# q and k transposed by VectorE in blocks of 32 and carried to their pixels' partitions by DMA, instead of by TensorE; their products one unit later

## The chip, the cores and the metric

The kernel runs on one core of a Trainium2 chip. The core has TensorE (PE, matrix products), VectorE (DVE), ScalarE (ACT), GpSimd (POOL) and SyncE (SP), each working through its own list of instructions in order, and 16 DMA engines that carry out the transfers which SP and ACT issue. The engines wait for each other through semaphores. The time is the device time from the first to the last instruction, in microseconds (us); the median of the runs counts. Less is better.

## The reference, cut to what matters

The input x is one image of 384 channels and 192 x 192 pixels. Two layers follow each other, each added to its input. The part that the change touches is in the first layer, after a group normalisation:

```python
qkv = jnp.einsum('bchw,oc->bohw', x, w_qkv) + b_qkv[None, :, None, None]
hs, ws = (h // DS, w // DS)                                   # DS = 2
qkv = qkv.reshape(b, 3 * c, hs, DS, ws, DS).max(axis=(3, 5))  # 96 x 96 pixels
qkv = lax.conv_general_dilated(qkv, w_dw, (1, 1), 'SAME', feature_group_count=3 * c, ...)
q, k, v = jnp.split(qkv, 3, axis=1)
...
q = q / jnp.clip(jnp.linalg.norm(q, axis=-1, keepdims=True), 1e-12)
k = k / jnp.clip(jnp.linalg.norm(k, axis=-1, keepdims=True), 1e-12)
attn = jnp.einsum('bhcn,bhdn->bhcd', q, k) * temperature[None]
```

So q, k and v are 384 channels each: a 1x1 product over the channels of x, the maximum over 2x2 pixels, and a 3x3 convolution of each channel by itself. The attention is between channels: for each of 8 heads of 48 channels, the product of q and k is a sum over all 9216 pixels. Four softmaxes over the largest entries of each row, weighted, then multiply v. A GELU, an enlargement to 192 x 192 and a 1x1 product finish the first layer; the second takes the signs of the normalised sum, shifts channels sideways and multiplies by the signs of a weight.

## The kernel before, in words

The image is cut into 24 units of 8 rows (1536 pixels) with the 384 channels as 3 blocks of 128 partitions. A unit of x is one load of 2304 KB into one of 8 buffers of the pool `big`. There are four stages:

1. all units are read once for the group sums (0 to 159 us), and the last six read are kept (`kept`);
2. all units again, for q and k (159 to 1408 us): this is the stage of the change;
3. all units a third time for v, with the softmaxes and the attention between (1408 to 1900 us);
4. the end of the first layer and the second layer, with the output (1900 us on).

In stage 2 the loop over units `u` calls `qkv_unit` for six channel blocks `m`: 0 to 2 are q, 3 to 5 are k. For each `m` PE makes three blocks of 512 columns, each of three matmuls over the input channels (line 316; an fp32 matmul shows in the profile as two passes). DVE takes the maximum over 2x2 pixels of each out of PSUM into `pooled` (line 323, three reductions). ACT adds the bias (line 330), and makes the first of nine taps of the 3x3 convolution (line 337) into a tile `dw`; DVE adds the other eight (line 339, eight instructions of 128 x 384). ACT then copies the last two pooled rows for the next unit (line 341) and sums the squares of `dw` for the norms (line 360). A unit gives 4 rows of 96 pixels, 384 columns; the first unit gives 3 rows, the last 5.

The product of q and k sums over pixels, and PE sums over partitions, so both are needed with pixels on the partitions. For each 128 columns, PE transposes the three q blocks into one PSUM tile `tr` and the three k blocks into another (line 367, against an identity matrix), ACT copies each to `qkT` (line 368), and PE makes three products of 144, 192 and 144 columns (line 371) that stay summed in three PSUM banks `gram` over the whole stage. PSUM's eight banks are three for `qkv`, two for `tr`, three for `gram`.

No order is written by hand in stages 1 to 3: a scheduler places each engine's instructions when the kernel is built, and puts the transposes and products of a unit between the matmuls of the next. PE's list has, for instance, the q transposes of a unit among the next unit's first matmuls. The loads of x in stages 2 and 3 stand on SP's list alone, each waiting for its buffer.

Of the kernel before, what the change touches and what calls it, by code (L numbers as in the profile page):

```python
# [10 lines left out]
F32 = mybir.dt.float32  # L11
# [3 lines left out]
BF16 = mybir.dt.bfloat16  # L15
# [3 lines left out]
PSUM = bass.MemoryType.PSUM  # L19

P = 128
C = 384
CT = C // P
# [9 lines left out]
NU = H // UR  # L33
UPX = UR * W
PR = UR // 2
# [5 lines left out]
LEAD = 4  # L41
SLEN = UR * PITCH
HALF = P // 2

STEP = 1584
SAT = [16 + t * STEP + t - SHIFT // 2 for t in range(CT)]
# [13 lines left out]
KEEP = 6  # L60
# [8 lines left out]
HEAD1 = [((t + 1) * P - 1) // HD for t in range(CT)]  # L69
D0 = [h * HD for h in HEAD0]  # L70
DN = [(h1 - h0 + 1) * HD for h0, h1 in zip(HEAD0, HEAD1)]
PAIR = 2 * HD
NP = C // PAIR
Q = P // NP
# [4 lines left out]
def shift_halves():  # L79
# [8 lines left out]
    for t in range(CT):  # L88
        other.append([])
        for h, (d, e) in enumerate(zip(shift[t], (shift[t][1], 0))):  # L90
            n = HALF - len(of[d])
            at[h * HALF : (h + 1) * HALF, t] = of[d][:REST] + of[e][:n] + of[d][REST:]
            of[e] = of[e][n:]
# [8 lines left out]
def pair_rows():  # L102
# [6 lines left out]
    for p in range(NP):  # L109
        v[p * Q : (p + 1) * Q] = p * PAIR + np.stack([i, HD + i, np.where(i < HD - Q, Q + i, 2 * Q + i)], 1)  # L110
    for t in range(CT):
        o[:PAIR, t] = t * PAIR + np.arange(PAIR)
        o[PAIR:, t] = CT * PAIR + t * Q + i
    assert sorted(v.flat) == sorted(o.flat) == list(range(C))
# [28 lines left out]
def conv_preact_kernel(ctx: ExitStack, tc: tile.TileContext, a: dict, out: bass.AP):  # L143
    nc = tc.nc
# [6 lines left out]
    big = ctx.enter_context(tc.tile_pool(name="big", bufs=NBIG))  # L151

    ident = const.tile([P, P], F32, name="ident")
# [18 lines left out]
    def unit(u, pool=big, parts=1):  # L172
        xt = pool.tile([P, CT, UPX], F32, name="xt", tag="big")
        n = CT // parts
        for t in range(0, CT, n):
            nc.sync.dma_start(xt[:, t : t + n], xv[u][:, t : t + n])
        return xt
# [24 lines left out]
    def right(name, bufs=1, stack=att):  # L202
        return stack.enter_context(tc.tile_pool(name=name, bufs=bufs, side="right"))
# [3 lines left out]
    ssq = ap.tile([P, 2 * CT, NU], F32, name="ssq")  # L207
    gsb = ap.tile([P, CT, max(DN)], F32, name="gsb")
    osum = ap.tile([P, CT, NAB], F32, name="osum")
# [4 lines left out]
    kept = {}  # L214
    with tc.tile_pool(name="p1", bufs=1, side="right") as p1, tc.tile_pool(name="p1ps", bufs=2, space=PSUM) as psp:
        stats = [p1.tile([P, CT, BATCH * (UPX // 512) * 6], F32, name=f"stats{i}") for i in range(NB)]
        mv = p1.tile([P, CT, NB, 2], F32, name="mv")
        acc = p1.tile([P, CT, 2, NU // SHARE], F32, name="acc")
        wg = p1.tile([NG, 3 * C], F32, name="wg")
        seen = 0  # L220
        for i in range(NU):
            u = NU - 1 - i
            xt = unit(u, parts=CT if u in (0, NU - 1) else 1)
# [13 lines left out]
            else:  # L237
                b, k = divmod(seen, BATCH)
                seen += 1
                for t in range(CT):  # L240
                    for j in range(UPX // 512):
                        at = (k * (UPX // 512) + j) * 6
# [3 lines left out]
            if u == NU // 2:  # L246

                for m in range(3):
                    ps = psp.tile([NG, C], F32, name="wgps")
# [7 lines left out]
        more = p1.tile([P, CT, 2], F32, name="more")  # L257
        nc.vector.tensor_reduce(more, acc, AX.X, ALU.add)
        sq = p1.tile([P, CT, NB], F32, name="sq0")
# [5 lines left out]
        ps = psp.tile([NG, 2], F32, name="gsps")  # L265
# [10 lines left out]
        ps = psp.tile([P, CT, 2], F32, name="spread")  # L276
# [9 lines left out]
        ps = psp.tile([P, NM], F32, name="bqps")  # L286
# [4 lines left out]
    def padded(pool, n):  # L291


        ts = []
        for m in range(n):
            t = pool.tile([P, PR + 3, WP + 2], F32, name=f"pooled{m}")
            nc.gpsimd.memset(t[:, 0:2, :], 0.0)  # L297
            nc.gpsimd.memset(t[:, 2 : PR + 2, 0:1], 0.0)
            nc.gpsimd.memset(t[:, 2 : PR + 2, WP + 1 :], 0.0)
            nc.gpsimd.memset(t[:, PR + 2 :, :], 0.0)  # L300
            ts.append(t)
        return ts

    def rows(u):

        return (1 if u else 2), (PR if u < NU - 1 else PR + 1)
# [36 lines left out]

    with tc.tile_pool(name="p2w", bufs=1, side="right") as wp, tc.tile_pool(
        name="p2t", bufs=2, side="right"
    ) as tp, tc.tile_pool(name="p2qkv", bufs=3, space=PSUM) as pqkv, tc.tile_pool(
        name="p2tr", bufs=2, space=PSUM
    ) as ptr, tc.tile_pool(name="p2g", bufs=1, space=PSUM) as pg:
        pool = padded(wp, 2 * CT)
        dwo = [wp.tile([P, (PR + 1) * WP], F32, name=f"dw{m}") for m in range(2 * CT)]  # L350
        gram = [pg.tile([P, 512], F32, name=f"gram{t}") for t in range(CT)]
        for u in range(NU):
            xt = kept.pop(u) if u in kept else unit(u)
            lo, hi = rows(u)
            n = hi - lo + 1
            for m in range(2 * CT):
                acc = dwo[m][:, : n * WP]
                qkv_unit(pqkv, xt, u, m, pool[m], [(acc, 0, n)])
                sq = tp.tile([P, (PR + 1) * WP], F32, name="sq", bufs=1)
                nc.scalar.activation(sq[:, : n * WP], acc, AF.Square, accum_out=ssq[:, m, u : u + 1])  # L360
            for c0 in range(0, n * WP, P):
                L = min(P, n * WP - c0)
                qkT = tp.tile([P, 2, C], F32, name="qkT")
                for s in range(2):
                    ps = ptr.tile([P, C], F32, name="tr")
                    for t in range(CT):
                        nc.tensor.transpose(ps[:L, t * P : (t + 1) * P], dwo[s * CT + t][:, c0 : c0 + L], ident)  # L367
                    nc.scalar.copy(qkT[:L, s, :], ps[:L, :])
                first, last = u == 0 and c0 == 0, u == NU - 1 and c0 + P >= n * WP
                for t in range(CT):  # L370
                    nc.tensor.matmul(  # L371
                        gram[t][:, : DN[t]],
                        qkT[:L, 0, t * P : (t + 1) * P],
                        qkT[:L, 1, D0[t] : D0[t] + DN[t]],
                        start=first,
                        stop=last,
                    )
        for t in range(CT):
            nc.vector.tensor_copy(gsb[:, t, : DN[t]], gram[t][:, : DN[t]])

    wpr = ctx.enter_context(tc.tile_pool(name="wpr", bufs=1)).tile([P, CT, C], F32, name="wpr")
    nc.scalar.dma_start(wpr, a["w_projT"].rearrange("(t p) o -> p t o", p=P))
    def softmaxes(p3, psp):
# [22 lines left out]
        for t in range(CT):  # L406
            g = gsb[:, t, : DN[t]]
            nc.vector.tensor_mul(g, g, rk[:, D0[t] : D0[t] + DN[t]])
            nc.vector.tensor_scalar_mul(g, g, rq[:, t : t + 1])
# [74 lines left out]
    def opened(name, bufs, **kw):  # L484
        return end.enter_context(tc.tile_pool(name=name, bufs=bufs, reuse_waits="tile", **kw))
# [19 lines left out]
    with ExitStack() as vs:  # L505
        wp = right("p4w", stack=vs)
        scratch = vs.enter_context(ExitStack())
        p3 = right("p3", stack=scratch)
        pqkv = vs.enter_context(tc.tile_pool(name="p4qkv", bufs=3, space=PSUM))
# [15 lines left out]
        def attention(g):  # L525
# [4 lines left out]
            for t in range(CT):  # L530
                for p in range(NP):
                    rows = slice(p * Q, (p + 1) * Q)
                    nc.tensor.matmul(  # L533
                        pss[p][:PAIR],
                        aT[rows, t, p * PAIR : (p + 1) * PAIR],
                        chunk[c][rows, t, cols],
# [8 lines left out]
        for u in range(NU):  # L545
            xt = unit(u)
# [6 lines left out]
            lo, hi = rows(u)  # L553
            first = PR * u - 2 + lo
            last = first + hi - lo
# [18 lines left out]
        with tc.manual_schedule():  # L574
# [10 lines left out]
            ps = psp.tile([P, P], F32, name="p3ps")[:NG, :1]  # L585
# [4 lines left out]
            ps = psp.tile([P, P], F32, name="p3ps")[:, :CT].unsqueeze(2)  # L590
# [6 lines left out]
    with end:  # L597
        more, sp = opened("p5x1", 1), opened("p5s", 1)
# [8 lines left out]
        def rows_of(ts, p, at=0, pitch=PITCH, n=W):  # L607
            return ts[p, at : at + UR * pitch].rearrange("p (r w) -> p r w", w=pitch)[:, :, :n]
# [18 lines left out]
        def moved(sg, t, h):  # L627

            d, n = OTHER[t][h]
            p = slice(h * HALF + REST, h * HALF + REST + n)  # L630
            src, to = SAT[t] - HSHIFT[t][h], SAT[t] - d
            by = rest[t % 2]
            nc.gpsimd.tensor_copy(
                rows_of(by.bitcast(I32), p, 0, PITCH // 4, W // 4),
                rows_of(sg.bitcast(I32), p, src // 4, PITCH // 4, W // 4),
            )
            if d:

                assert to % 4 == 0
                nc.gpsimd.tensor_copy(sg.bitcast(I32)[p, to // 4 : (to + SLEN) // 4], by.bitcast(I32)[p])  # L640
            elif to % 2 == 0:
                nc.gpsimd.tensor_copy(
                    rows_of(sg.bitcast(U16), p, to // 2, PITCH // 2, W // 2),
                    rows_of(by.bitcast(U16), p, 0, PITCH // 2, W // 2),
                )
            else:
                nc.gpsimd.tensor_copy(rows_of(sg, p, to), rows_of(by, p))  # L647

        def signed(i):

            xt, sg = kept[order[i]], signs[i % NSIGN]
            for k in range(2 * CT):
                t, h = divmod(k, 2)
                p = slice(h * HALF, (h + 1) * HALF)
                nc.scalar.activation(  # L655
# [47 lines left out]
        with tc.manual_schedule():  # L703
            v = todo.pop(0)
# [85 lines left out]
```

## Time and profile before

The time before is 2334.4 us, the median of three runs (2333.51 to 2335.75); the profiled run has a span of 2331.7 us. Busy time over the span:

| engine | busy us | share | instructions |
|---|---|---|---|
| PE | 2154.3 | 92% | 6573 |
| DVE | 1824.6 | 78% | 3113 |
| ACT | 878.3 | 38% | 1564 |
| POOL | 209.3 | 9% | 337 |

The groups that the change touches or leans on, over the whole run:

| line, engine | what | count | busy us | mean ns |
|---|---|---|---|---|
| 316 PE | qkv, 128x512 | 3888 | 1700.1 | 593 |
| 367 PE | transposes, 128x128 | 438 | 74.3 | 279 |
| 339 DVE | taps of q and k, 128x384 | 1152 | 709.5 | 616 |
| 323 DVE | maximum over 2x2 | 648 | 443.3 | 685 |
| 368 ACT | copies to qkT, 128x384 | 146 | | 475 |

How to read it: busy time of PE is not time at its peak, and matmuls overlap, so the step from one start to the next says more than the length of one. In a timeline line the columns are start, length (us), engine, line, operation, output<-inputs, shape and count, and in brackets the idle time before it and what ended that. In a line of waits they are who waited for whom, us in total, how often, and the longest. In the windows each stretch has its length, and for each engine its busy time and number of instructions, then the granted clock of PE (1.00 is full), the share of the DMA engines and GB/s.

### The profile page before, as it was taken

To read this page: it belongs to the slowest core of one execution; us is meant where nothing else is said; L and a number is where in the kernel's file an instruction comes from. 1 tells how busy PE (TensorE), PEld (TensorE's weight loads), DVE (VectorE), ACT (ScalarE), POOL (GpSimd) and SP (SyncE) were. 2 spreads that over 40 slices of the span, in tenths; PEclk is the share of its full clock that TensorE was granted. 3 is DMA by queue.
4 is the path that set the end of the run, shared out by engine and by line. 5 is a ranking of instruction groups with operands and counts; after the bars stand their busy time and mean duration, and the time that the engine had idled before them with its cause. 6 is when DMAs were issued, how large, how long until landed. Compare 5 with 4: busy or idle time off the path is not lost.

```text
span 2331.7 us, 19363 instructions
## 1 busy us (share of the span) xinstructions
PE 2154.3 (92%) x6573; PEld 1028.9 (44%) x6573; DVE 1824.6 (78%) x3113; ACT 878.3 (38%) x1564; POOL 209.3 (9%) x337
## 2 busy tenths in 40 slices
PE   1039999999999999999999999999999999999998
PEld 0024444445444444444444444443444444455554
DVE  4657777777777777777777788987787887888998
ACT  5432322223222223322322222225333233497775
POOL 0000000000000000000000000000000000186674
PEclk7569999999999999999999999999999999999999
DMA  9961111121111111110111113105221312289995
GB/s 399 418 269 41 41 41 41 43 79 41 41 41 41 41 41 65 58 41 0 41 41 41 41 41 112 41 0 203 82 81 41 122 41 81 82 325 393 412 411 243
DMA packets 47443, 271.54 MB, mean 116 GB/s; under 512 B 2256, under 2 KB 3568, under 8 KB 47344
## 3 DMA queue, kind: packets, MB, share of 16 engines
q1 hardware_dynamic: 36656, 214.70, 23.6%
q10 hardware_dynamic: 10688, 55.61, 5.9%
q8 instruction: 51, 0.84, 0.1%
q14 instruction: 48, 0.39, 0.0%
HBM read 213.68 MB, written 56.62 MB: 116 GB/s over the span
## 4 chain that ended last, share of the span: by engine, by line
PE 48%; DVE 34%; ACT 9%; DMA 7%; issue 2%; SPq 0%; ACTq 0%; POOLq 0%; POOL 0%; DVEq 0%
PE qkv L316 34%; DVE dw L339 18%; DVE pooled L323 9%; DMA xt<-in_x_dram 6%; PE l1ps L675 5%; DVE chunk L339 4%; PE yps L493 3%; ACT pooled L330 3%; ACT dw L337 3%; PE gram L371 3%; PE ops L533 2%; PE tr L367 2%; DVE xt L502 2%; ACT sq L360 2%; ACT signs L655 1%
## 5 line engine op out<-in xcount | busy, mean ns | idle before, releaser
L316 PE MATMUL qkv<-xt,wq 128*128 128x512 f32 x3888 | 1700.1, 593 | 0.3 <-DVE small L289 0.3
L316 PEld LDWEIGHTS qkv<-xt,wq 128*128 128x128 f32 x3888 | 726.1, 190 | 862.3 <-issue 797.0
L339 DVE SCALAR_TENSOR_TENSOR dw<-pooled,small,dw 128x384 f32<-128x384 f32 (+2 forms) x1152 | 709.5, 616 | 251.4 <-ACT dw L337 226.9
L323 DVE TENSOR_REDUCE pooled<-qkv 128x128 f32<-128x512 f32 x648 | 443.3, 685 | 78.5 <-PE qkv L316 72.2
L339 DVE SCALAR_TENSOR_TENSOR chunk<-pooled,small,chunk 128x384 f32<-128x384 f32 (+3 forms) x696 | 370.8, 547 | 73.4 <-ACT chunk L337 56.0
L341 ACT COPY pooled<-pooled 128x196 f32<-128x196 f32 x207 | 73.7, 356 | 743.4 <-DVE dw L339 520.6
L330 ACT ACTIVATE pooled<-pooled,small 128x384 f32<-128x384 f32 x216 | 133.2, 617 | 331.8 <-DVE pooled L323 331.8
L655 ACT ACTIVATE signs<-xt,nmean 64x1536 fp8e4<-64x1536 f32 x144 | 226.5, 1573 | 64.6 <-PE yps L493 52.1
L675 PE MATMUL l1ps<-signs,wb 128*128 128x384 fp8e4 x864 | 151.5, 330 | 5.5 <-POOL signs L647 4.5
L502 DVE SCALAR_TENSOR_TENSOR xt<-yps,small,xt 128x768 f32<-128x768 f32 x132 | 127.9, 1013 | 25.9 <-PE yps L493 21.3
L493 PE MATMUL yps<-chunk,wpr 128*128 128x384 f32 x396 | 138.2, 495 | 6.7 <-DVE xt L502 6.7
L683 DVE SCALAR_TENSOR_TENSOR xt<-l1ps,small,xt 128x768 f32<-128x768 f32 x144 | 135.7, 1009 | 7.1 <-ACT signs L655 4.0
L360 ACT ACTIVATE sq<-dw 128x384 f32<-128x384 f32 (+2 forms) x144 | 75.3, 523 | 158.1 <-DVE dw L339 158.1
L243 DVE BATCH_NORM_STATS2 stats<-xt 128x6 f32<-128x512 f32 x144 | 87.2, 676 | 58.8 <-DMA xt<-in_x_dram 58.8
L297 POOL MEMSET pooled<- 128x196 f32 x9 | 2.4, 267 | 1402.0 <-PE tr L367 1244.3
L675 PEld LDWEIGHTS <-wb 128*128 128x128 fp8e4 x864 | 84.5, 98 | 74.0 <-issue 16.5
L193 PE MATMUL gsps<-sums,small 128*32 128x2 f32 x6 | 0.5, 196 | 125.8 <-DVE sums L264 125.8
L337 ACT ACTIVATE dw<-pooled,small 128x384 f32<-128x384 f32 (+2 forms) x144 | 100.8, 700 | 30.3 <-PE tr L367 28.1
L493 PEld LDWEIGHTS yps<-chunk,wpr 128*128 128x128 f32 x396 | 73.4, 192 | 62.8 <-PE yps L493 16.4
L234 ACT ACTIVATE junk<-xt 128x1536 bf16<-128x1536 f32 x48 | 71.1, 1482 | 51.0 <-DMA xt<-in_x_dram 49.8
L367 PEld LDWEIGHTS tr<-ident,dw 128*128 128x128 f32 (+2 forms) x438 | 52.2, 140 | 70.5 <-DVE dw L339 31.1
L367 PE MATMUL tr<-ident,dw 128*128 128x128 f32 (+2 forms) x438 | 74.3, 279 | 8.9 <-DVE dw L339 8.1
(117 smaller groups left out, 765.9 us busy)
## 6 DMA issues: line engine op xcount, KB each, us to landing
xt<-in_x_dram SPq DMA_DIRECT2D x83, 2304.0 KB, 13.4
out_dram<-xt ACTq DMA_DIRECT2D x19, 2304.0 KB, 13.8
xt<-in_x_dram SPq DMA_DIRECT2D x18, 768.0 KB, 8.2
out_dram<-xt ACTq DMA_DIRECT2D x9, 768.0 KB, 7.6
out_dram<-xt SPq DMA_DIRECT2D x6, 768.0 KB, 6.6
wq<-in_w_qkvT_dram ACTq DMA_DIRECT2D x1, 1728.0 KB, 15.2
wl<-in_w_projG_dram ACTq DMA_DIRECT2D x1, 576.0 KB, 3.8
wpr<-in_w_projT_dram ACTq DMA_DIRECT2D x1, 576.0 KB, 5.1
```

Of the source, the lines that this page charges most:

```text
L316: nc.tensor.matmul(ps, wq[:, t, m * P : (m + 1) * P], x4[:, t, r0 : r0 + nr, c0 : c0 + ncol], start=(t == 0), stop=(t == CT - 1),)
L323: nc.vector.tensor_reduce(pl[:, 2 + r0 // 2 : 2 + (r0 + nr) // 2, 1 + c0 // 2 : 1 + (c0 + ncol) // 2], ps.rearrange("p (i a j b) -> p i j ...
L330: nc.scalar.activation(new, new, AF.Identity, bias=bq[:, m : m + 1])
L337: nc.scalar.activation(acc2, src, AF.Identity, bias=bdw[:, m : m + 1], scale=wdw[:, m, 0:1])
L339: nc.vector.scalar_tensor_tensor(acc2, src, wdw[:, m, k : k + 1], acc2, ALU.mult, ALU.add)
L360: nc.scalar.activation(sq[:, : n * WP], acc, AF.Square, accum_out=ssq[:, m, u : u + 1])
L367: nc.tensor.transpose(ps[:L, t * P : (t + 1) * P], dwo[s * CT + t][:, c0 : c0 + L], ident)
L493: nc.tensor.matmul(ps, wpr[:, t, m * P : (m + 1) * P], o[:, t, :], start=(t == 0), stop=(t == CT - 1),)
L502: nc.vector.scalar_tensor_tensor(x5[:, m, r], yb, bpr[:, m : m + 1], x5[:, m, r], ALU.add, ALU.add)
L655: nc.scalar.activation(rows_of(sg, p, SAT[t] - HSHIFT[t][h]), xt[p, t, :].rearrange("p (r w) -> p r w", w=W), AF.Sign, bias=nmean1[p, t : ...
L675: nc.tensor.matmul(ps[:, j, : 2 * W], wb[:, t, m * P : (m + 1) * P], rows_of(sg, slice(0, P), SAT[t])[:, r0 + 2 * j : r0 + 2 * j + 2], sta ...
L683: nc.vector.scalar_tensor_tensor(blk, ps[:, :, : 2 * W], bl1[:, m : m + 1], blk, ALU.add, ALU.add)
```

## The change

PE no longer transposes q and k, and ACT no longer copies the results. Instead, as soon as a channel block's taps are done, DVE transposes it in blocks of 32 x 32 (`transposed`): within each group of 32 partitions, 32 channels of 32 pixels become 32 pixels of 32 channels. This leaves the pixels of column group j still on the partitions of their channel group i. DMA then carries each such piece to the partitions 32 j to 32 j + 31 (`moved`): 16 transfers for q after `m` = 2 and 16 for k after `m` = 5, all issued by SP, of pieces of 128 bytes for q and 384 bytes for k. They land in `qkT`, which lies in one of the eight buffers of `big` (`room`), so one fewer is left for x. `products` multiplies a unit's q and k in the middle of the next unit. The slices of k are taken in whole blocks of 32 channels (`B0`, `BN`), so the products have 160, 192 and 160 columns.

What it is for: PE is relieved of the transposes, and the two PSUM banks of `tr` go to `qkv`, which has five. Beside this, `dw` is a tile of two buffers instead of six tiles, the squares' output `sq` is bf16, and loads of x are asked for up to six units ahead (`KEEP`), since their place in SP's list is now among the moves.

```diff
+B = 32
+NBP = P // B
...
+B0 = [d // B for d in D0]
+BN = [-(-(d + n) // B) - b for d, n, b in zip(D0, DN, B0)]
...
-    ) as tp, tc.tile_pool(name="p2qkv", bufs=3, space=PSUM) as pqkv, tc.tile_pool(
-        name="p2tr", bufs=2, space=PSUM
-    ) as ptr, tc.tile_pool(name="p2g", bufs=1, space=PSUM) as pg:
+    ) as tp, tc.tile_pool(name="p2qkv", bufs=5, space=PSUM) as pqkv, tc.tile_pool(
+        name="p2g", bufs=1, space=PSUM
+    ) as pg:
...
+        blocks = wp.tile([P, 2, size], F32, name="blocks")
+        nc.gpsimd.memset(blocks, 0.0)
+        room = big.tile([P, CT, UPX], F32, name="room", tag="big").rearrange("p t n -> p (t n)")
+        qkT = room[:, : 2 * size].rearrange("p (s n) -> p s n", s=2)
...
+        def transposed(u, s, t, acc):
+            n, nk, *_ = of_unit(u)
+            to = blocks[:, s, : nk * C].rearrange("p (j t k c) -> p t k j c", j=NBP, t=CT, c=B)[:, t]
+            full, more = divmod(n * WP // B, NBP)
+            nc.vector.transpose(to[:, :full], acc[:, : full * P].rearrange("p (k j c) -> p k j c", j=NBP, c=B))
+            if more:
+                src = acc[:, full * P : n * WP].rearrange("p (j c) -> p j c", c=B)
+                nc.vector.transpose(to[:, full, :more], src)
+
+        def moved(u, s):
+
+            n, nk, q, k = of_unit(u)
+            for j in range(NBP):
+                src = blocks[:, s, j * nk * CT * B : (j + 1) * nk * CT * B]
+                for i in range(NBP):
+                    at, to = slice(i * B, (i + 1) * B), slice(j * B, (j + 1) * B)
+                    if s == 0:
+                        nc.sync.dma_start(
+                            q[to].rearrange("p t k (i c) -> p i (t k) c", i=NBP)[:, i],
+                            src[at].rearrange("p (m c) -> p m c", c=B),
+                        )
+                    else:
+                        nc.sync.dma_start(
+                            k[to].rearrange("p (t i) k c -> p i t (k c)", i=NBP)[:, i],
+                            src[at].rearrange("p (t m) -> p t m", t=CT),
+                        )
...
         for u in range(NU):
-            xt = kept.pop(u) if u in kept else unit(u)
+            for v in range(u, min(u + KEEP + 1, NU)):
+                if v not in kept:
+                    kept[v] = unit(v)
+            xt = kept.pop(u)
...
             for m in range(2 * CT):
-                acc = dwo[m][:, : n * WP]
+                acc = tp.tile([P, (PR + 1) * WP], F32, name="dw")[:, : n * WP]
                 qkv_unit(pqkv, xt, u, m, pool[m], [(acc, 0, n)])
-                sq = tp.tile([P, (PR + 1) * WP], F32, name="sq", bufs=1)
+                transposed(u, *divmod(m, CT), acc)
+                sq = tp.tile([P, (PR + 1) * WP], BF16, name="sq", bufs=1)
                 nc.scalar.activation(sq[:, : n * WP], acc, AF.Square, accum_out=ssq[:, m, u : u + 1])
-            for c0 in range(0, n * WP, P):
-                L = min(P, n * WP - c0)
-                qkT = tp.tile([P, 2, C], F32, name="qkT")
-                for s in range(2):
-                    ps = ptr.tile([P, C], F32, name="tr")
-                    for t in range(CT):
-                        nc.tensor.transpose(ps[:L, t * P : (t + 1) * P], dwo[s * CT + t][:, c0 : c0 + L], ident)
-                    nc.scalar.copy(qkT[:L, s, :], ps[:L, :])
...
+                if u and m == CT - 1:
+                    products(u - 1)
+                if m % CT == CT - 1:
+                    moved(u, m // CT)
+        products(NU - 1)
```

More of the change, by code (lines that the diff above doesn't have):

```diff
@@ L345, in conv_preact_kernel, with of_unit, products @@
         name="p2t", bufs=2, side="right"
-    ) as tp, tc.tile_pool(name="p2qkv", bufs=3, space=PSUM) as pqkv, tc.tile_pool(
-        name="p2tr", bufs=2, space=PSUM
-    ) as ptr, tc.tile_pool(name="p2g", bufs=1, space=PSUM) as pg:
+    ) as tp, tc.tile_pool(name="p2qkv", bufs=5, space=PSUM) as pqkv, tc.tile_pool(
+        name="p2g", bufs=1, space=PSUM
+    ) as pg:
         pool = padded(wp, 2 * CT)
-        dwo = [wp.tile([P, (PR + 1) * WP], F32, name=f"dw{m}") for m in range(2 * CT)]
         gram = [pg.tile([P, 512], F32, name=f"gram{t}") for t in range(CT)]
+        size = -(-(PR + 1) * WP // P) * C
+        blocks = wp.tile([P, 2, size], F32, name="blocks")
+        nc.gpsimd.memset(blocks, 0.0)
+        room = big.tile([P, CT, UPX], F32, name="room", tag="big").rearrange("p t n -> p (t n)")
+        qkT = room[:, : 2 * size].rearrange("p (s n) -> p s n", s=2)
+        def of_unit(u):
+            lo, hi = rows(u)
+            n = hi - lo + 1
+            nk = -(-n * WP // P)
+            q, k = qkT[:, 0, : nk * C], qkT[:, 1, : nk * C]
+            return (
+                n,
+                nk,
+                q.rearrange("p (t k c) -> p t k c", t=CT, k=nk),
+                k.rearrange("p (b k c) -> p b k c", k=nk, c=B),
+            )
[22 more added lines that the diff above has]
+                            src[at].rearrange("p (t m) -> p t m", t=CT),
+                        )
+        def products(u):
+            n, nk, q, k = of_unit(u)
+            for i in range(nk):
+                L = min(P, n * WP - i * P)
+                for t in range(CT):
+                    nc.tensor.matmul(
+                        gram[t][:, : BN[t] * B],
+                        q[:L, t, i],
+                        k[:L, B0[t] : B0[t] + BN[t], i],
+                        start=u == 0 and i == 0,
+                        stop=u == NU - 1 and i == nk - 1,
+                    )
@@ L356, in conv_preact_kernel @@
             for m in range(2 * CT):
-                acc = dwo[m][:, : n * WP]
+                acc = tp.tile([P, (PR + 1) * WP], F32, name="dw")[:, : n * WP]
                 qkv_unit(pqkv, xt, u, m, pool[m], [(acc, 0, n)])
-                sq = tp.tile([P, (PR + 1) * WP], F32, name="sq", bufs=1)
+                transposed(u, *divmod(m, CT), acc)
+                sq = tp.tile([P, (PR + 1) * WP], BF16, name="sq", bufs=1)
                 nc.scalar.activation(sq[:, : n * WP], acc, AF.Square, accum_out=ssq[:, m, u : u + 1])
-            for c0 in range(0, n * WP, P):
-                L = min(P, n * WP - c0)
-                qkT = tp.tile([P, 2, C], F32, name="qkT")
-                for s in range(2):
-                    ps = ptr.tile([P, C], F32, name="tr")
-                    for t in range(CT):
-                        nc.tensor.transpose(ps[:L, t * P : (t + 1) * P], dwo[s * CT + t][:, c0 : c0 + L], ident)
-                    nc.scalar.copy(qkT[:L, s, :], ps[:L, :])
[L369 to L377, printed above, removed]
+                if u and m == CT - 1:
[3 more added lines that the diff above has]
+        products(NU - 1)
         for t in range(CT):
-            nc.vector.tensor_copy(gsb[:, t, : DN[t]], gram[t][:, : DN[t]])
+            at = D0[t] - B0[t] * B
+            nc.vector.tensor_copy(gsb[:, t, : DN[t]], gram[t][:, at : at + DN[t]])
     wpr = ctx.enter_context(tc.tile_pool(name="wpr", bufs=1)).tile([P, CT, C], F32, name="wpr")
```

## The prediction

> **What bounds the kernel now.** I read first the windows of the stages. 159 to 1408 us is the stage of q and k, the only one the diff touches; 1408 to 1900 is the stage of v.
>
> ```profile
> core 0: us, PE busy (x) PEld busy (x) DVE busy (x) ACT busy (x) POOL busy (x), PEclk, DMA share, GB/s
> ...
> 211.00:1408.00 1197.00, 1187.58 (x3366) 572.36 (x3365) 915.53 (x1530) 356.12 (x830) 2.27 (x14) 1.00 0.12 43
> 1408.00:1900.00 492.00, 490.25 (x1395) 210.69 (x1394) 408.56 (x875) 161.53 (x363) 0.10 (x1) 1.00 0.21 80
> ```
>
> PE is busy 99% at full clock, DVE 76%, the DMA engines 12%. Next, the timeline of PE over one unit, from its first transpose at 464.32 to the next unit's at 515.79: a period of 51.47 us.
>
> ```profile
> 464.32 0.60 PE L367 MATMUL tr<-ident,dw 128*128 128x128 f32 x4
> ...
> 466.36 0.44 PE L367 MATMUL tr<-ident,dw 128*128 128x128 f32 x2 [0.36 <-DVE dw L339]
> ...
> 474.92 1.79 PE L371 MATMUL gram<-qkT 128*128 128x144 f32 x12
> 476.55 0.82 PE L367 MATMUL tr<-ident,dw 128*128 128x128 f32 x6
> 477.21 1.88 PE L316 MATMUL qkv<-xt,wq 128*128 128x512 f32 x4
> 478.93 0.98 PE L371 MATMUL gram<-qkT 128*128 128x144 f32 x6
> 479.74 36.21 PE L316 MATMUL qkv<-xt,wq 128*128 128x512 f32 x84
> 515.79 0.60 PE L367 MATMUL tr<-ident,dw 128*128 128x128 f32 x4
> ```
>
> Start to start, 84 qkv passes take 36.05 us, 0.429 each; a unit has 108 (54 fp32 matmuls, two passes each): 46.35. The 18 products take 1.63 + 0.81 = 2.44. What is left, 2.68 us, is the 18 transposes with their waits. Then the timelines of DVE and ACT around one block's end, and DVE's waits over the stage.
>
> ```profile
> 457.20 0.68 DVE L323 TENSOR_REDUCE pooled<-qkv 128x128 f32<-128x512 f32 x1
> 457.81 0.61 DVE L339 SCALAR_TENSOR_TENSOR dw<-pooled,small,dw 128x384 f32<-128x384 f32 x1
> 459.69 0.62 DVE L339 SCALAR_TENSOR_TENSOR dw<-pooled,small,dw 128x384 f32<-128x384 f32 x1 [1.28 <-ACT dw L337]
> ```
> ```profile
> 457.92 0.62 ACT L330 ACTIVATE pooled<-pooled,small 128x384 f32<-128x384 f32 x1 [1.50 <-DVE pooled L323]
> 458.45 0.52 ACT L360 ACTIVATE sq<-dw 128x384 f32<-128x384 f32 x1
> 458.88 0.19 ACT L360 ACTIVATION_READ_ACCUMULATOR sq<-dw 128x1 f32 x1
> 458.97 0.69 ACT L337 ACTIVATE dw<-pooled,small 128x384 f32<-128x384 f32 x1
> ```
> ```profile
> DVE dw L339 <- ACT dw L337: 218.4, 136, 3.1
> ...
> DVE pooled L323 <- PE qkv L316: 34.0, 47, 3.9
> ```
>
> DVE's 24% idle isn't free room: after each block's third reduction it waits through three ACT steps. Per unit it works 48 taps x 0.61 + 18 reductions x 0.605 = 40.2 us (steps start to start), waits 218.4 / 23.3 units = 9.4 for ACT, and only 34.0 / 23.3 = 1.5 for PE. So PE is the bound with 1.5 us to spare per unit, and any work put on DVE has to fall into the ACT waits.
>
> [...] No transpose of DVE is in this trace. [...] the moves are pieces of 128 and 384 B. The trace has none so short with data: its shortest, 880 B, took 41 ns each on their engine. [...] in the line below 24 packets of 65 ns per engine are 1.6 of the 3.8 us, which leaves 2.2.
>
> ```profile
> wl<-in_w_projG_dram ACTq DMA_DIRECT2D x1, 576.0 KB, 3.8
> ```
>
> **The change, part by part.**
>
> *PE.* The transposes and their waits go: -2.68 us a unit. The products widen from 144, 192, 144 to 160, 192, 160 columns, 512 for 480, so 2.44 becomes 2.60. New PE period: 46.35 + 2.60 = 48.95. The two banks of `tr` go to `qkv`, five instead of three, so PE can run 5 x 2.58 = 12.9 us ahead of DVE. The products wait on eight DMA semaphores; at 0.02 to 0.05 us each (the semaphore events of the trace), hidden or at most 0.4 us a unit; I take them as hidden behind running matmuls.
>
> *DVE.* Six transposes of 128x384 fp32 per unit. Nearest row: a tap of the same shape, 0.61 us. [...] I take 0.6: +3.6 us. Its place decides what this costs. From a third reduction's next issue slot to the first tap DVE needs 1.905 us (0.605 + 1.28, and the 0.02 between), or 1.375 where ACT's square is already behind it. In the built order, between the two stand: for channel blocks 1 and 2 a tap, the transpose and a reduction (1.815, gap 0.09); for block 3 nothing (1.375); for 4 the transpose (gap 0.775); for 5 and 0 a tap and the transpose (gap 0.695 each). Gaps: 3.7. DVE's period: 40.2 + 3.6 + 3.7 = 47.5. At 1.0 us a transpose: 40.2 + 6.0 + 2.3 = 48.5. Both stay under 48.95. ACT loses six copies of 0.475 us a unit, which also delayed the ACT chain.
>
> *Moves.* 16 for q and 16 for k per unit, all on SP's queue with the load of x between them; each holds SP some 0.37 us (the loads' median), and each waits for the landing of the eighth before it. Engine time per unit: 18 pieces for each q move, 6 for each k move, 384 pieces an engine; at 14 ns (880 B in 41 ns and 1536 in 65 give 9 + 0.037 per byte) 5.3 us, at 82 (twice the 880 B packet) 31 us, both under 48.95. What matters is the wait at the products. k's last transpose stands after the third reduction of the next unit, 3 x 2.58 + 1.4 = 9.2 us after PE ends the unit. The 16 k moves take 16 x 0.37 + 2.3 = 8.2, so all has landed at 17.4; PE reaches the products after 28 to 30 matmuls, at 24.1 or later. Seven us to spare; the load of x (issued when PE ends the unit, 8.1 us to land) is mostly through by 9.2. q's moves follow the products and have half a unit. So: off the path.
>
> *The end of the stage.* The last unit has 480 columns: taps of 0.71, and two transpose instructions for each channel block (0.9). From PE's start of that unit, DVE stands at 9.6 after block 0, then has 15 reductions (9.1), 48 taps (34.1), 6 x 0.9 and gaps of 3.0: done at 61.2, which is 12.2 after PE's 48.95. The k moves land 8.2 later, at 20.4. PE has three blocks of v (7.7) ahead of the last products, and then stands for 12.7 us (8 to 18), with the whole v stage, PE-bound at 490.25 of 492, behind it in the queue. The next loads of x, queued behind those moves on SP, arrive before v's second unit.
>
> *Sum.* Before: 159.22 to 1407.07 (v's continuous run on PE), 1247.85, of it qkv 2592 x 0.429 = 1112.5, products 73 column blocks x 0.813 = 59.4, slow clock at the start 1.6, so transposes with waits 74.3. After: 1112.5 + 73 x 0.867 + 1.6 + 12.7 = 1190. Saved 57: 2334.4 - 57 = **2277**.
>
> **Rivals.** *DVE becomes the bound.* For it: the margin is 1.4 us in 49, the period rests on ACT's turns, and a 4-byte transpose isn't in the trace. Against: the gaps take up most of a transpose. At 1.4 us each: 40.2 + 8.4 + 1.4 = 50.0, so 24 x 1.05 = 25 more, and 2 for a longer last lag: 2304. *The moves come late and PE stands at every product.* For it: 32 small DMAs a unit, eight in flight, [...] and SP's in-order queue; against: the 2.2 us fixed part and 7 us of room. If each move took as long to land as the 2304 KB loads (13.4 us), 16 would be two rounds, 26.8: 9.2 + 26.8 - 24.1 = 11.9 us a unit, x 23 = 274: 2551, far slower. Break-even lies where the k moves need 17.4 us, 1.1 each. *The end costs more:* if v's second load and DVE's backlog stretch the stand to 30 us, 2294.
>
> **How the numbers follow.** PE-bound with a short stand 0.60; longer stand at the end 0.10; DVE-bound 0.18; late moves 0.12. Best possible is no stand and nothing exposed, 2264. Range 2262 to 2306 leaves out the late moves and little else. Faster by over 0.2%: 0.87; within: 0.02; slower: 0.11.
>
> **What would show it.** Right: in the q and k stage PE periods near 49.0 us with no idle ahead of the products except the last; DVE transposes of 0.5 to 0.7 us; DVE's waits for ACT falling from 9.4 to about 4 us a unit; k moves landing in 8 to 10 us; one PE idle of 8 to 18 us near 1340. Wrong: PE waiting for DVE's reductions (DVE-bound), or for DMA at each product.

## The result and the profile after

The changed kernel takes 2299.36 us (2297.71 to 2301.02, four runs) beside 2333.95 for the kernel before (2331.95 to 2335.75, four runs): a ratio of 0.9852, 95% interval 0.9835 to 0.9869. It is 34.6 us faster; 57 were forecast, 2277 with a range of 2262 to 2306.

First the windows: the stage of q and k, and the 50 us around its end. Columns as in the prediction.

```profile
211.00:1340.00 1129.00, 1127.40 (x2901) 532.22 (x2900) 985.31 (x1664) 298.73 (x687) 0.00 (x0) 1.00 0.23 62
1340.00:1390.00 50.00, 30.14 (x82) 16.23 (x81) 20.42 (x45) 5.03 (x10) 2.37 (x14) 0.80 0.73 276
```

Over the stage PE now has 1127.40 of 1129 us, 99.9% against 99.2%, although DVE went from 76% to 87%. At the end of the stage it works only 30 of 50 us, and at a mean clock of 0.80. Those are the two findings of this case: a steady part that went as worked out, and an end that didn't.

The timeline of PE over one unit in the steady part:

```profile
479.85 2.77 PE L410 MATMUL gram<-room 128*128 128x160 f32 x18
482.45 46.51 PE L321 MATMUL qkv<-xt,wq 128*128 128x512 f32 x108
528.80 2.77 PE L410 MATMUL gram<-room 128*128 128x160 f32 x18
```

No idle stands in brackets, and from product to product it is 48.95 us: 46.35 for 108 passes and 2.60 for 18 products. Before, it was 51.47.

DVE around a block's end, then its group of transposes over the whole run (count | busy us, mean ns | idle ahead), then its waits from 211 to 1330 us:

```profile
455.77 0.58 DVE L381 STREAM_TRANSPOSE blocks<-dw 128x384 f32<-128x384 f32 x1
457.02 0.62 DVE L344 SCALAR_TENSOR_TENSOR dw<-pooled,small,dw 128x384 f32<-128x384 f32 x1 [0.67 <-ACT dw L342]
...
458.16 1.92 DVE L344 SCALAR_TENSOR_TENSOR dw<-pooled,small,dw 128x384 f32<-128x384 f32 x3
459.99 0.68 DVE L328 TENSOR_REDUCE pooled<-qkv 128x128 f32<-128x512 f32 x1
```
```profile
L381 DVE STREAM_TRANSPOSE blocks<-dw 128x384 f32<-128x384 f32 x138 | 79.3, 575 | 3.2
```
```profile
DVE dw L344 <- ACT dw L342: 86.6, 92, 1.5
DVE pooled L328 <- PE qkv L321: 30.4, 64, 0.9
```

A transpose lasts 0.575 us, and it stands in the gap that ACT's chain leaves: the wait after it is 0.67, where the block shown before waited 1.28. Per unit (1119 / 48.95 = 22.9 of them) DVE waits 3.8 us for ACT, down from 9.4, and still 1.3 for PE.

SP's list in one unit, and the page's line of the moves (KB of each, us from issue to landing):

```profile
464.28 10.22 SPq L399 DMA_DIRECT2D room<-blocks  x16
486.99 10.43 SPq L394 DMA_DIRECT2D room<-blocks  x16
```
```profile
room<-blocks SPq DMA_DIRECT2D x736, 36.0 KB, 2.0
```

Sixteen moves hold SP for 10.2 us, 0.64 each from start to start, not 0.37. The k moves have landed at about 476.5, 3.4 us before the products at 479.85.

Now the end of the stage. PE, then DVE, then SP and ACT:

```profile
1337.05 7.99 PE L321 MATMUL qkv<-xt,wq 128*128 128x512 f32 x18 [1.60 <-DVE pooled L328]
1357.49 6.04 PE L410 MATMUL gram<-room 128*128 128x160 f32 x24 [12.45 <-DMA room<-blocks]
1363.36 1.02 PE L321 MATMUL qkv<-xt,wq 128*128 128x512 f32 x2
1371.80 0.48 PE L198 MATMUL p3ps<-small 128*32 128x1 f32 x6 [7.41 <-DVE gsb L438]
...
1400.15 0.49 PE L460 MATMUL p3ps<-dg,ones 128*128 128x128 f32 x2 [1.61 <-DVE dg L458]
```
```profile
1345.56 0.23 DVE L384 STREAM_TRANSPOSE blocks<-dw 128x96 f32<-128x96 f32 x1
1357.66 1.89 DVE L328 TENSOR_REDUCE pooled<-qkv 128x128 f32<-128x512 f32 x3 [11.87 <-DMA room<-blocks]
...
1369.69 1.35 DVE L575 TENSOR_REDUCE wg<-wl 128x96 f32<-128x1152 f32 x1 [8.24 <-DMA wl<-in_w_projG_dram]
1370.96 0.78 DVE L438 COPY gsb<-gram 128x144 f32<-128x144 f32 x3
```
```profile
1345.66 10.25 SPq L399 DMA_DIRECT2D room<-blocks  x16
1355.96 33.31 SPq L181 DMA_DIRECT2D xt<-in_x_dram  x6
```
```profile
1357.59 0.44 ACTq L574 DMA_DIRECT2D wl<-in_w_projG_dram  x1
```

PE stands 12.45 us for the moves, as foreseen. But DVE waits for the same moves before its first reduction of v, which has nothing to do with q or k; ACT issues the load of `wl` only at 1357.59; and once DVE goes on, it stands another 8.24 us for `wl`, with the copies of `gram` (`gsb`) queued behind it and PE behind those.

The kernel before had a wait of the same kind at this place:

```profile
1405.69 1.29 DVE L323 TENSOR_REDUCE pooled<-qkv 128x128 f32<-128x512 f32 x2 [5.95 <-PE tr L367]
```

There too v's first reductions waited, 5.95 us, until the last reader of a tile of q and k (`dw`, read by the transposes) was done, and `wl` was issued right then, at 1405.68. It cost PE nothing, since PE was busy with those transposes, and `wl` landed in 3.8 us.

### The profile page after: what moved, and what is told of

The parts are those of the page before. It is cut to its first block, busy times and chain, and to the rows that moved or that the text cites. A ratio compares the mean times of both kernels' runs of the same rounds, so it can differ in the third digit from the quotient of the medians.

```text
span 2297.4 us, 19469 instructions
## 1 busy us (share of the span) xinstructions
PE 2104.5 (92%) x6135; PEld 995.6 (43%) x6135; DVE 1903.4 (83%) x3269; ACT 819.2 (36%) x1418; POOL 211.2 (9%) x338
## 4 chain that ended last, share of the span: by engine, by line
PE 75%; DVE 11%; DMA 9%; ACT 2%; issue 1%; SPq 1%; ACTq 0%; POOLq 0%; POOL 0%; DVEq 0%
PE qkv L321 63%; DMA xt<-in_x_dram 6%; PE l1ps L734 4%; DVE chunk L344 4%; PE yps L552 3%; PE gram L410 3%; DVE pooled L328 2%; PE ops L592 2%; DVE xt L561 2%; DVE dw L344 1%; DMA out_dram<-xt 1%; ACT signs L714 1%; DVE stats L248 1%; DMA wl<-in_weightT_dram 1%; DMA wl<-in_w_projG_dram 1%
## 5 line engine op out<-in xcount | busy, mean ns | idle before, releaser
L321 PE MATMUL qkv<-xt,wq 128*128 128x512 f32 x3888 | 1682.8, 594 | 1.9 <-DVE pooled L328 1.6
L321 PEld LDWEIGHTS qkv<-xt,wq 128*128 128x128 f32 x3888 | 736.4, 190 | 922.4 <-issue 824.5
L430 ACT ACTIVATE sq<-dw 128x384 bf16<-128x384 f32 (+2 forms) x144 | 75.3, 523 | 116.9 <-DVE dw L344 116.9
L381 DVE STREAM_TRANSPOSE blocks<-dw 128x384 f32<-128x384 f32 (+1 forms) x144 | 82.0, 569 | 3.5
L410 PE MATMUL gram<-room 128*128 128x160 f32 (+3 forms) x438 | 69.9, 315 | 12.4 <-DMA room<-blocks 12.4
## 6 DMA issues: line engine op xcount, KB each, us to landing
xt<-in_x_dram SPq DMA_DIRECT2D x83, 2304.0 KB, 14.9
wq<-in_w_qkvT_dram ACTq DMA_DIRECT2D x1, 1728.0 KB, 14.9
```

What stands on the lines that cost most here:

```text
L321: nc.tensor.matmul(ps, wq[:, t, m * P : (m + 1) * P], x4[:, t, r0 : r0 + nr, c0 : c0 + ncol], start=(t == 0), stop=(t == CT - 1),)
L410: nc.tensor.matmul(gram[t][:, : BN[t] * B], q[:L, t, i], k[:L, B0[t] : B0[t] + BN[t], i], start=u == 0 and i == 0, stop=u == NU - 1 and i ...
```

## The experiments

The theory after reading this: the tile `blocks` lies in the pool `p2w`, whose memory the v stage takes over for `pooled` and `wl`. So v's first reductions and the load of `wl` wait until the last move has read `blocks`, and `wl`, issued late, arrives behind the loads of x that SP has just issued. Rivals: the moves themselves hold up the end, and two queues would cure it; or DVE or the moves are the bound of the steady part. The times given are medians, each compared with runs of the kernel before on the same chip (2333.1 to 2334.1).

**A pool of its own for `blocks`.**

```diff
-    ) as pg:
+    ) as pg, tc.tile_pool(name="p2b", bufs=1, side="right") as pb:
-        blocks = wp.tile([P, 2, size], F32, name="blocks")
+        blocks = pb.tile([P, 2, size], F32, name="blocks")
```

> Only the memory of the tile blocks changes: it gets a pool of its own, so that the tiles of the v stage (pooled, wl) no longer wait for the last k move to release their memory. In the built order PE then has 7 blocks of v, not 3, ahead of the last products. Theory (the late k moves of the last unit hold PE, DVE and the loads of wl because blocks' memory is shared with the v stage): PE's stand of 12.5 us before the last products shrinks to some 4 us in two pieces, the 7.4 us before the product with small and the 11 us wait for weightT vanish; 2299 - 21 = 2278. Rival (it is the queue of x loads ahead of wl, or the data itself, not the memory): both waits stay, at most 5 us gained, 2294 or more.

2274.77 us, ratio 0.9748 (0.9735 to 0.9762): 24.6 below the changed kernel, without touching a move. The timeline of PE in this run, then DVE after its last transpose:

```profile
1336.96 7.99 PE L321 MATMUL qkv<-xt,wq 128*128 128x512 f32 x18 [1.60 <-DVE pooled L328]
1346.40 10.57 PE L321 MATMUL qkv<-xt,wq 128*128 128x512 f32 x24 [1.45 <-DVE pooled L328]
1357.75 3.71 PE L410 MATMUL gram<-room 128*128 128x160 f32 x24 [0.77 <-DMA room<-blocks]
```
```profile
1345.70 1.85 DVE L328 TENSOR_REDUCE pooled<-qkv 128x128 f32<-128x512 f32 x3
```

The moves are issued and land when they did before (products at 1357.75 instead of 1357.49), but PE now has seven blocks of v ahead of the products instead of three, since DVE reads v's banks at once (1345.70 instead of 1357.66), and the stand is 0.77 us. In this run `wl` is issued at 1345.2, before SP's loads of x (1355.9), and lands in 4.1 us. The clock stays at 1.00 from 1340 to 1390 us. The memory that `blocks` shares is the cause of the loss: with it apart, the stand and the late `wl` are both gone. Whether v's tiles lie on the bytes of `blocks` itself or only in the same pool is not told apart by this.

**The last k moves on two queues**, with `blocks` where the change has it:

```diff
+                    eng = nc.scalar if u == NU - 1 and s and i % 2 else nc.sync
-                        nc.sync.dma_start(
+                        eng.dma_start(
```

> For the last unit alone, every second k move is issued by ACT instead of SP. Theory (16 issues of 0.64 us each on one queue are 10.2 of the 12.2 us between the last transpose and the landing): 8 issues take 5.1, PE's stand falls from 12.5 to about 7.4 us, and the later waits stay; 2299 - 5 = 2294. Rival (the transfers themselves are slow): stand unchanged, 2299.

2297.00, ratio 0.9842 (0.9828 to 0.9855). The stand went from 12.45 to 7.90, about as expected, and the wait of PE for `gsb` grew from 7.41 to 8.42, with `wl` still landing 12 us after its issue. Only 2.4 us of the time went. In the profiled run more was gained up to stage 4, which begins 3.8 us earlier than in the changed kernel (its first product on PE at 1992.52 for 1996.36); but stage 4 took 294.5 us for 292.8. No edit here touches stage 4, and over the profiled runs of this document it takes 290.3 to 294.8 us, so 1 or 2 us between two kernels can come from there alone.

**Both together.** The two edits above.

> The two edits together: blocks in a pool of its own, and the last unit's k moves on two queues. PE has 5 blocks of v ahead of the last products in the built order. Theory: with the memory freed, PE's stand is hidden behind v blocks whether the moves take 12 or 7 us, so as the first edit alone within 3 us: 2276 to 2280. Rival (the two gains add): 2278 - 5 = 2273 or less.

2291.74, ratio 0.9825 (0.9812 to 0.9838). The expectation fell: it is 17 slower than the own pool alone. PE of this run, then the load of `wl` (duration in ns, start of the first and last):

```profile
1369.65 0.48 PE L198 MATMUL p3ps<-small 128*32 128x1 f32 x6 [9.68 <-DVE gsb L439]
```
```profile
L575 ACTq DMA_DIRECT2D wl<-in_w_projG_dram x1: 546/546/546, 1353.1 to 1353.1; - x1
```

ACT had eight moves to issue before `wl`, so `wl` left at 1353.1 instead of 1345.2, after SP had begun its loads of x at 1352.6, and took 13.6 us to land. Tested below with `wl` out of the way.

**Three banks for `qkv` instead of five.** `bufs=5` to `bufs=3` in the pool `p2qkv`.

> As the changed kernel, but qkv has three PSUM banks as before instead of five; two stay unused. Theory (the gain is PE's shorter list; DVE keeps pace with 1.5 us to spare per unit): unit period stays at 48.95 us or up to 49.3, 2299 to 2307. Rival (the two banks, which let PE run further ahead, are the gain): period back to 51 us or more, 2340 or more.

2298.89, ratio 0.9853 (0.9839 to 0.9866): no change, with the same period of 48.95. The freed banks gain nothing in this kernel; what the steady part gains is PE's own time.

**Each transpose done twice.**

```diff
-                transposed(u, *divmod(m, CT), acc)
+                for _ in range(2):
+                    transposed(u, *divmod(m, CT), acc)
```

> Every DVE transpose is done twice, with the same result. From the changed kernel's trace: DVE works 43.8 us of a unit's 48.95, waits 3.8 for ACT and 1.3 for PE; a transpose holds DVE for 0.50 us. Theory (DVE's work falls into its waits for ACT): work 46.8, the waits for ACT shrink to 2.2, sum 49.0, so PE stays the bound or nearly, plus some 4 us at the last unit: 2299 to 2315. Rival (DVE work adds in full): 6 x 0.50 x 24 = 72 more, 2371.

2303.34, ratio 0.9866 (0.985 to 0.9883). DVE's busy time from 400 to 1300 us rises from 785.06 to 841.00, 0.51 us for each added transpose, and its waits for ACT fall from 86.6 to 40.7; PE's period stays at 48.95. The 4 us more come at the end of the stage: PE's wait there for a reduction is 3.54 instead of 1.60, and the last transpose is later.

**Each transpose done three times** (`range(3)`).

> Every DVE transpose is done three times, with the same result. Theory (the waits for ACT are used up and DVE becomes the bound): work 49.8 and the 1.4 us of the one wait that nothing covers, 51.2 us a unit, 2.3 over the present, x 24 and 8 at the end: about 2360. Rival one (DVE work adds in full): 144 more, 2443. Rival two (DVE's 5 us of idle time are free room): 6.0 - 5.1 = 0.9 a unit, 2320.

2320.42, ratio 0.9944 (0.9924 to 0.9964, two runs), far less than the theory gave. It is the number of the second rival, but not by that rival's sum, which had 0.9 us a unit and nothing at the end. The windows of this run, 400 to 1300 us, a piece of DVE's timeline, and PE ahead of one unit's products:

```profile
400.00:1300.00 900.00, 890.60 (x2281) 417.20 (x2281) 859.09 (x1524) 238.69 (x545) 0.00 (x0) 1.00 0.23 61
```
```profile
626.34 0.58 DVE L381 STREAM_TRANSPOSE blocks<-dw 128x384 f32<-128x384 f32 x1
626.85 0.58 DVE L344 SCALAR_TENSOR_TENSOR dw<-pooled,small,dw 128x384 f32<-128x384 f32 x1
627.34 0.57 DVE L381 STREAM_TRANSPOSE blocks<-dw 128x384 f32<-128x384 f32 x1
```
```profile
682.86 2.84 PE L410 MATMUL gram<-room 128*128 128x160 f32 x18 [0.93 <-DMA room<-blocks]
```

PE's period is now 49.60 us in the mean (21 units, 287.30 to 1328.84 us), 0.65 more than in the changed kernel. PE stands 9.4 of 900 us, ahead of the products: the k moves come late because DVE does. DVE's waits for ACT are down to 27.0. So about here DVE becomes the bound, with some 6 us of transposes a unit added. The theory counted them in full, but DVE's busy time rose by only 4.6 us a unit (859.09 / 18.15 units against 785.06 / 18.38). In this order many transposes stand between taps, and a tap there takes 0.49 us from start to start (626.85 to 627.34), where three in a row of one block take 0.61 each (458.16 to 459.99 above). PE ends its last qkv pass of q and k 14.2 us later than in the changed kernel (1349.63 for 1335.45); the rest comes at the end, where PE waits 5.82 us for a reduction before its stand.

**All q moves issued twice** (`moved` called again for q).

> Every q move is issued twice, with the same result: 16 more transfers a unit, 10.3 us more of SP's queue. Theory (q's moves have half a unit of room): the queue is free again before the load of x and k's moves are due, 2299 within 4. Rival (the moves load the DMA engines or SP enough to matter): 2310 or more.

2299.46, ratio 0.9854 (0.984 to 0.9869): the same time as the change. q's moves are hidden: in one unit SP issues the 32 of them from 636.5 to 657.4 us, and k's begin at 660.9. The products stand 6 to 18 passes later in PE's list than in the changed kernel, since the order was worked out anew.

**All k moves issued twice.**

> Every k move is issued twice, with the same result. In the changed kernel k's moves are issued from 464.3 to 474.5 us, land by 476.5, and PE reaches the products at 479.85: 3.4 us of room. Theory: 10.2 us more leaves PE standing 6.9 us at every product, x 23, and 10 more at the end: about 2465. Rival (PE runs ahead through its five banks and hides it): 2299 to 2310.

2310.19, ratio 0.99 (0.988 to 0.992, two runs), not 2465. PE in the steady part is busy 900.00 of 900. SP's 32 k moves now take 21 us, but in this kernel the products stand 32 to 42 passes later in PE's list (14 to 18 us): the scheduler moved them behind the longer transfer, which the expectation had held in place. So the steady margin of 3.4 us isn't a cliff as long as the order is worked out anew; what the same moves cost with the order kept was not tried. At the end there is no later work to move behind, and there the cost shows, in PE:

```profile
1368.91 5.15 PE L410 MATMUL gram<-room 128*128 128x160 f32 x24 [22.28 <-DMA room<-blocks]
```

9.8 us more than 12.45, for 16 moves more: about 0.6 each, once.

**`wl` loaded early**, from a pool of its own opened ahead of stage 2, with `blocks` left in `p2w`:

```diff
+    wlp = right("wlp")
+    wl = wlp.tile([P, CT, C], F32, name="wl")
+    nc.scalar.dma_start(wl, a["w_projG"].rearrange("(t p) o -> p t o", p=P))
...
-        wl = wp.tile([P, CT, C], F32, name="wl")
-        nc.scalar.dma_start(wl, a["w_projG"].rearrange("(t p) o -> p t o", p=P))
```

> As the changed kernel, but wl has memory of its own from before the q and k stage, so that both its loads and what is made from them move to the start of that stage; blocks still shares memory with the v stage. Theory (two separate losses at the stage's end: PE stands for the k moves because DVE may not touch the v stage's memory, and then the loads of wl arrive 12 us late behind four loads of x): the stand of 12.5 us before the products stays, the 7.4 us before the product with small and the 2 us of the products with dg go: 2299 - 10 = 2289. Rival (one loss, the stand): 2297 or more.

2286.82, ratio 0.9803 (0.9789 to 0.9817), 12.5 below the change. The stand for the moves is still there (13.28), and the waits for `gsb` and `dg` are gone. Of the 12.5 us, 1.4 is not from the end: the stage of q and k begins at 159.43 instead of 160.87. So there are two losses, and the two edits take them apart: some 11 us for the late `wl`, some 12 to 13 for the stand.

**Own pool and early `wl`.** The edits of both.

> Both: blocks in a pool of its own and wl loaded early. With the own pool alone wl was issued before the loads of x and cost PE nothing, so theory: nothing more to gain there, 2275 within 3. Rival (wl still costs through ACT and DVE): 2270 or less.

2272.69, ratio 0.9741 (0.9727 to 0.9755): the fastest of all, 61 us below before, but only 2 below the own pool alone, which already brings `wl` in time; 1.7 of these 2 us is again the earlier start of the stage (159.18 for 160.86).

**The same with the last k moves on two queues.**

> Own pool, the last unit's k moves on two queues, and wl loaded early. The same without the early wl took 2292. Theory (there the k moves on ACT's queue pushed the load of wl behind the loads of x, which landed 13 us later): with wl early, the 9.7 us before the product with small and some 5 us after it go: 2275 within 3. Rival (the moves on ACT's queue do harm by themselves, through ACT's work behind them): 2285 or more.

2275.97, ratio 0.9753 (0.9739 to 0.9767): 15.8 below the same kernel with the late `wl`. So what slowed that one was the order of ACT's list, not the moves. Two queues bring nothing once the stand is covered (2272.69 without them).

**The kernel before with the two side edits** (loads of x asked for six units ahead, `sq` in bf16) and PE's transposes kept.

> The kernel before with two of the change's side edits alone: loads of x asked for up to six units ahead, and the squares' output in bf16. Theory (they gain nothing by themselves): 2333 within 4. Rival (they carry part of the gain): 2325 or less.

2333.59, ratio 0.9999 (0.999 to 1.0008). The gain isn't theirs.

## Why the prediction was right in direction and 22 us too low

*PE's period, 48.95.* Exact. The DMA waits at the products cost nothing that shows: no idle stands ahead of the products at 479.85.

*DVE.* 0.6 was taken for a transpose, an estimate beside the tap of the same shape (0.61), since the trace of before holds no transpose of DVE; 0.575 was measured, 0.50 to the next start (1345.06 to 1345.56 us in the changed kernel). The gaps for ACT were put at 3.7 a unit and measured at 3.8. The rival that DVE becomes the bound fell, with more room than the 1.4 us given: doubling the transposes (3 us) left the period as it was.

*The moves.* The piece cost came out at the low end of the span of 14 to 82 ns: median 11 ns for a piece of 128 B and 24 for 384. With 288 and 96 pieces an engine that is 5.5 us a unit, for 5.3 at the low end. It makes 12 and 16 GB/s of an engine, beside 26 for the 6144 B pieces of x (234 ns). The prediction's line from longer pieces, 9 ns and 0.037 per byte, gives 14 and 23 for these two sizes, so it held for them within 3 ns. The 2.2 us fixed, worked out from the load of `wl`, agrees with a landing of 2.0. What was too low is SP's time per issue, taken from the loads of x: 0.64 for 0.37, so 16 k moves take 12.2 with landing, not 8.2, and the spare time was 3.4 us, not 7. Still off the path, so the rival of late moves fell. Its break-even was misread as well: 17.4 us is when the moves were to have landed; they may take 24.1 - 9.2 = 14.9. The forecast did not rest on it.

*The end of the stage, the step that failed.* "PE has three blocks of v (7.7) ahead of the last products, and then stands for 12.7 us": 12.45 was measured, and yet the working behind it doesn't hold. DVE was done 10.3 us after PE's last qkv of q and k (1335.45 to 1345.8), not 12.2; the moves needed 11.7 more, not 8.2; and v's three blocks, 8.0 us of work, began 1.6 late. So 10.3 + 11.7 - 1.6 - 8.0 = 12.4 stands where 12.2 + 8.2 - 7.7 = 12.7 was worked out: that they agree is luck. And only three blocks of v stand ahead of the products because v's matmuls have three PSUM banks (`p4qkv`) and DVE, held by the memory of `blocks`, empties none of them; with that memory apart there are seven, and the stand is gone. The step saw one wait, of PE, and priced the next stage behind it as free of the change. It wasn't. The losses that it leaves out, in the changed kernel:

| loss | us | from |
|---|---|---|
| PE waits for `gsb`, behind `wl` | 7.4 | timeline of PE |
| products after the stand: 5.87 for 24 (1357.49 to 1363.36) where 2.60 x 24 / 18 = 3.47 | 2.4 | timeline of PE |
| the next 52 qkv passes: 24.2 for 22.3 | 1.9 | 1372.20 to 1396.43 |
| two waits for `dg` | 2.0 | 1.61 and 0.36 |
| DVE late for the last reductions of the stage | 1.6 | timeline of PE |
| sum | 15.3 | |

The slow products are the clock. At the end of the stage the granted clock of the changed kernel was about half in these two stretches (third figure from the end):

```profile
1348.60:1362.20 13.60, 4.71 (x16) 4.74 (x17) 3.45 (x10) 1.32 (x3) 2.37 (x14) 0.50 0.58 178
1369.00:1375.90 6.90, 4.10 (x11) 2.02 (x12) 4.37 (x13) 0.35 (x1) 0.00 (x0) 0.51 1.02 415
```

PE stopped at 1345.04 and its clock was halved 3.6 us later; PE started again at 1357.49 and the clock was back 4.7 us later. The second window follows PE's idle time from 1364.4 to 1371.8. In the kernel with `blocks` in its own pool, which has no such stand and a clock of 1.00 from 1340 to 1390, the same 24 products take 3.55 (1357.75 to 1361.30). With `wl` early and the stand still there, what went at the end was about 11 us, as the rows for `gsb`, `dg` and the 52 passes add up to (11.3).

*The sum.* A second fault is arithmetic. The before-stage was measured to 1407.07, but by then PE had already done 18 passes of v's work among the last transposes, 7.7 us. They were counted as "transposes with waits", 74.3, which should be 66.6. The steps as they stood give 1247.85 - 1190.1 - 7.7 = 50.1 saved, where 57 was written, and with the 15.3 of the table 34.8. The same fault is in the best possible, 2264: without any stand it should have been some 2272, and the kernel with the own pool and the early `wl` took 2272.69 (with three short waits of PE left at its end, 3.6 us in all). Between the two traces, v's attention (`ops`) begins 31.9 us earlier, and q and k's stage itself began 1.65 later, so 33.6 was saved between: 1.2 below that sum. The spans differ by 34.3, so 2.4 more came in stage 4, which the change does not touch and which scatters by more than that between kernels.

*The rival "the end costs more"* (2294) is the nearest to the time measured, and it had the right place but not the cause: it made the stand itself 30 us long, from v's second load and DVE's backlog. The stand stayed at 12.45, and the rest came as separate waits behind it. That 2299 lies within the range at all is owed to the room left for such rivals (2294, and 2304 for DVE), not to the sum.

## What to carry to other kernels

Where a tile becomes the source of DMA moves, ask whether the next stage takes over its memory, and if so give the tile memory that nothing claims at once: here v's first reduction stood 11.87 us until the last move had landed. That one edit was worth 24.6 of the 58 us that the kernel then saves. The trace of before can show the place: a wait there that costs nothing (5.95 us here) may be lengthened by the change. At the end of a stage, follow not the one engine that waits but every engine's list: `wl`, issued 8 to 12 us late here, fell among four large loads and landed in 12.1 to 13.6 us instead of 4.1. And when a before-stage is timed by a start mark, count what the next stage has already done by then.

## What the runs showed of the hardware

- In the changed kernel a 36 KB move of many pieces held SP for 0.60 us (k) and 0.61 us (q), in the median; a load of x held it for 0.42 there and for 0.37 in the kernel before. The moves' pieces, from SBUF to SBUF, took 11 ns (128 B) and 24 ns (384 B), for 234 ns for the 6144 B pieces of a load of x.
- A 576 KB load landed in 4.1 us when ACT issued it 11 us before SP began four 2304 KB loads (own pool for `blocks`), and in 11.3 to 13.6 us when it was issued after SP had begun them. In the changed kernel the DMA engines were busy for 0.99 of the time in which it landed, at 398 GB/s (1357.60 to 1369.70 us); in the kernel before for 0.58, at 184 GB/s, and it landed in 3.8 us (1405.70 to 1409.50).
- With each transpose done twice, DVE took 3 us more a unit without lengthening the period of 48.95: the wait for ACT shrank instead (86.6 to 40.7 us over the stage).
- A tap on DVE took 0.61 us from start to start in a row of taps on one tile (changed kernel, 458.16 to 459.99), and 0.49 between two transposes (each done three times, 626.85 to 627.34).
